# A hybrid block on one Trainium2 core: rows turned through memory instead of through TensorE in the scan stage

## The chip, the core and the metric

The kernel runs on one core of a Trainium2 chip. The core has five engines with instruction streams of their own: PE (TensorE: matrix products into the PSUM memory), DVE (VectorE), ACT (ScalarE), POOL (GpSimd) and SP (SyncE, which here only issues DMAs). Each engine takes its instructions in the order in which the compiled program holds them; they meet through semaphores. SP and POOL issue the DMAs, each on a queue of its own, and 16 DMA engines carry both.

The metric is the device time of one execution in microseconds (us). Ten runs of the kernel before took 1613.59 to 1618.41 us, with a median of 1616.53 us.

## What is computed

Eight sequences of 512 tokens of width 256 pass four sublayers, each added to its input after a layer norm: a linear scan, a mixture of experts, a causal attention with 16 heads, and the same mixture again.

```python
x = x + scan(layernorm(x), Win, bin_, Bp, Cp, Dp, Wout, bout)
x = x + mixture(layernorm(x), router_w, bias, gate_w, up_w, down_w, sh_gate_w, sh_up_w, sh_down_w)
x = x + attention(layernorm(x), Wqkv, Wout)
x = x + mixture(layernorm(x), ...)
# scan:    xi = silu(x @ Win + bin_);  h = 0.9 * h + xi * Bp;  y = sum(h * Cp) + Dp * xi;  y @ Wout + bout
# mixture: scores = sigmoid(x @ router_w.T); the best 2 of 4 groups, of them the best 4 of 16 experts;
#          sum over those experts of weight * (silu(x @ gate) * (x @ up)) @ down, plus two experts that all tokens use
```

## The kernel before

**Stages.** The kernel runs four stages one behind the other: `stretch(Scan())`, `routed(0, ...)`, `stretch(Attention())` and `routed(1, ...)`. A stretch computes a sequence layer for all eight sequences, routes its result to the experts and computes the shared experts beside it; `routed` then runs the routed experts in blocks of 128 rows. The change touches the first stretch.

**Steps of the scan stretch.** A loop over `b` handles one sequence per step. Step `b` interleaves, on the engines, work on four different sequences:

- `layer.main(b, ...)`: the scan of sequence `b`. Eight pairs of products give `pz` (L563) from the turned rows `xT`, ACT and DVE make the states and `y` from it, and `add_projection` (L510, L519) multiplies by the output matrix and adds to the tile `x`.
- For the next sequence, `nxt = b + 1`: its load, its layer norm (`norm(nxt)`, DVE writes `xn`, L493), and `turn(nxt)`, which puts the normalised rows into the turned layout `xT` that the next step's `main` starts from.
- For the sequence before, `b - 1`: `start_route` stores `x` to memory (L1444), `r.norm()` writes its normalised rows into a tile of sorted rows (`sorted_m`, L493), `r.scores()` turns them, makes the router logits (`pl`, L669) and the scores, and `r.rest` goes on: five picks up to the choice `sel` (L739), the prefix product over tokens `pr` (L747, L748), the places and the weights of each choice, and 16 indirect DMAs by POOL (L798) that send rows to their experts' regions. `r.rest` runs on into the next step: its prefix product and the two pieces behind it stand at 0.10, 0.14 and 0.18 of step `b + 1`, the sends after them.
- For the sequences further back: a share of the two shared experts (`experts(layer.quota[...])`, L1146, L1174); 10 of 12 pieces of a sequence per step.

**Order.** `beside(...)` merges these pieces: every piece yields how much of its columns it has used, and the piece that is furthest behind goes next. `timed(steps, *places)` lets the steps of a piece start at given shares of the step (0 to 1). So a place is a share of the PE columns of the step, and sets the order of the text. The framework's compile-time planner then makes each engine's order from the text, with its own expectation of when each operand is there; on the chip that order is fixed, and an engine whose next instruction lacks an operand stands still. `tc.issue_after(...)` adds an order on one engine.

**Two ways of turning rows.** `turned` (L418 to L433) uses PE: for each half of the width four products with the identity matrix (128x128, L430) into one PSUM bank, and a copy of the bank to a tile, which the scan gives to ACT (L432). `by_shares` (L435 to L456) goes by way of memory: SP writes the rows (512 KB) to a DRAM tile `through` (L440), waits for that to land, reads them back in four DMAs of 128 KB (L443), arranged such that the blocks of 32x32 stand where a transposition of blocks alone makes the whole transposition, and DVE turns them in two instructions (L452). If `into_rows` is true the read comes into the tile that was written from; else into another tile of the pool `kb4`, of which there are nine. Before the change only the attention stretch uses `by_shares`, through these two lines, one in `turn` and one in the loop:

```python
if i == 1 and b >= layer.ahead:
    return by_shares(lambda: xn.pop(b), f"l{i}_{b}", lambda xnT: xT.update({b: xnT}), True)
...
timed(r.scores(i == 1), *scores[:2], *spread(*scores[2:], NT)),
```

**SP's queue in a step.** Besides the store of `x`, SP issues the load of a sequence that is needed later (`load_x`, L149), which takes the buffer of sequence `b - 1` (the pool has three) as soon as DVE has read that for `sorted_m`; behind it, by `issue_after`, in steps 2 to 5 six loads of expert weights of 256 KB each (L235 to L237) and one of zeros; and the sum of the shared experts of a sequence (L1184).

**The last step and the tail.** In step 7 the route of sequence 6 has tighter places (`last_rows`, `last_scores`), its picks stand at 0.57 to 0.76, and its prefix product and the two pieces behind it at 0.79, 0.81 and 0.83. After the loop the tail routes sequence 7: 20 pieces of the shared experts, the last four sends of sequence 5, the sends of sequence 6 from 0.16 on, the norm, scores and choice of sequence 7; then the rest of the shared experts beside the last sends and the table of expert blocks (`blocks`).

Of the kernel before, what the change touches and what calls it, by code (L numbers as in the profile page):

```python
# [19 lines left out]
NT = T // P  # L20
# [11 lines left out]
EG, TKG, TK = 4, 2, 4  # L32
# [50 lines left out]
def tile_hybrid_block(  # L83
# [276 lines left out]
    def behind(*pieces):  # L360
        def steps():
            for piece in pieces:
                yield from piece.steps

        return Piece(sum(piece.columns for piece in pieces), steps())
# [17 lines left out]
    def timed(steps, *places):  # L383


        def scaled():
            now = 0
            for place in places:
                yield place - now
                now = place  # L390
                next(steps)
            for _ in steps:
                pass

        return Piece(1, scaled())

    def spread(first: float, last: float, many: int):
        return [first + (last - first) * k / many for k in range(many)]

    def some(steps, many: int):  # L400

        for _ in range(many):
            yield next(steps)

    def issue(piece):
        for _ in piece.steps:
            pass
# [51 lines left out]
    by_scalar = (nc.scalar.copy, nc.scalar.copy)  # L459
# [60 lines left out]


    class Scan:
        mixture, ahead, copies, turns = 0, 1, by_scalar, (0.75, 0.79)
        quota = (10, 10, 20)
        over, sent, begun_last = 4, 0, 4
        early = 0


        norms, scores, choose = (0.08, 0.2, 0.32, 0.4), (0.53, 0.57, 0.65, 0.69), (0.71, 0.97)
        last_rows, last_scores = (0.26, 0.33), (0.43, 0.46)  # L530

        def load(self, b: int):
# [667 lines left out]
    class Attention:  # L1200
        mixture, ahead, copies, turns = 1, 2, by_both, (0.65, 0.85)
        quota = (10, 8, 20)
        over, sent, begun_last = 0, 4, 8
        early = 2
        norms, scores, choose = (0.0, 0.12, 0.2, 0.28), (0.29, 0.45, 0.55, 0.6), (0.66, 0.95)
        last_rows, last_scores = (0.2, 0.28), (0.35, 0.38)
# [214 lines left out]
    def stretch(layer):  # L1421


        i = layer.mixture
        xT, xn, made, routes, sends = {}, {}, {}, {}, []
# [6 lines left out]
            return normed(b, f"l{i}_{b}", place, False, first)  # L1432

        def turn(b: int, copies=layer.copies):
            if i == 1 and b >= layer.ahead:
                return by_shares(lambda: xn.pop(b), f"l{i}_{b}", lambda xnT: xT.update({b: xnT}), True)
            return turned(lambda: xn.pop(b), f"l{i}_{b}", lambda xnT: xT.update({b: xnT}), copies)

        def project(b: int):
            made[b], piece = layer.project(b, xT.pop(b))  # L1440
            return piece
# [12 lines left out]
        def experts(many: int):  # L1454
            return Piece(many * each, some(whole, many))
# [39 lines left out]
        def start_route(b: int):  # L1495
            routes[b] = Route(i, b, layer.copies)
            store(b)
            return routes[b]
# [4 lines left out]
        for b in range(1 if begun else 0, B):  # L1503
            pieces = [begun or layer.main(b, made.pop(b))]
            begun = None
            nxt, last = b + layer.ahead, b == B - 1
            scores, choose, turns = layer.scores, layer.choose, layer.turns
            if i == 0 and b == 1:

                scores, choose, turns = (0.95, 0.955, 0.97, 0.975), (0.98, 0.99), (0.96, 0.965)  # L1510
            fill = []
            if layer.ahead > 1 and not last:
                fill.append(project(b + 1))
            if b > 1:
                shared_sum = experts(layer.quota[last])
                fill.append(shared_sum)
                if len(sends) > 1:
                    pieces.append(timed(sends.pop(0), *spread(0.0, 0.16, layer.over)))
                wait = 0.16 if i == 0 and b == 2 else 0.0
                first = [wait + place for place in (0.1, 0.14, 0.18)]  # L1520
                if layer.over:
                    pieces.append(timed(some(sends[0], 3 + NT * TK - layer.over), *first, *spread(0.22 + wait, 0.97, NT * TK - layer.over)))
                else:
                    pieces.append(timed(sends.pop(), *first, *spread(0.22, 0.66 if last else 0.86, NT * TK)))
            if fill:
                pieces.append(behind(*fill))
            if b > 0:
                r = start_route(b - 1)
                if last:
                    pieces.append(timed(r.norm(), *spread(0.0, 0.12, NT), *spread(*layer.last_rows, NT)))  # L1530
                else:
                    first, then, rows, full = layer.norms
                    pieces.append(timed(r.norm(), *spread(first, then, NT), *spread(rows, full, NT)))
                sends.append(r.rest)
                if last:
                    pieces += [
                        timed(r.scores(), *layer.last_scores, *spread(0.5, 0.56, NT)),
                        timed(some(r.rest, PICKS), *spread(0.57, 0.67, PICKS - 1), 0.76),
                        timed(some(r.rest, 3 + layer.sent), 0.79, 0.81, 0.83, *spread(0.85, 1.0, layer.sent)),
                    ]  # L1540
                else:
                    pieces += [
                        timed(r.scores(i == 1), *scores[:2], *spread(*scores[2:], NT)),
                        timed(some(r.rest, PICKS), *spread(*choose, PICKS)),
                    ]
            if nxt < B:
                added = layer.load(nxt)
                if added is not None:
                    pieces.append(timed(added, 0.31, 0.34))
                stats = 0.36 if added is not None else 0.32  # L1550
                pieces += [
                    timed(norm(nxt), *spread(stats, 0.44, NT), *spread(0.56, 0.64, NT)),
                    timed(turn(nxt), *turns),
                ]
            issue(beside(*pieces))
            if layer.ahead == 1 and nxt < B:
                issue(project(nxt))
            if i == 0 and b == 2:
                for make in pending:
                    make()  # L1560
# [4 lines left out]
        r = start_route(B - 1)  # L1565
        chain = 3 + PICKS
        many = layer.begun_last
        left = [timed(sends.pop(0), *spread(0.0, 0.14, layer.over))] if layer.over else []
        within = (0.16, 0.8) if layer.over else (0.0, 0.5)
        issue(  # L1570
            beside(
                experts(layer.quota[2]),
                timed(r.norm(by_vector=True), *spread(0.0, 0.05, 2 * NT)),
                *left,
                timed(sends.pop(), *spread(*within, NT * TK - layer.sent)),
                timed(r.scores(), 0.2, 0.22, *spread(0.28, 0.33, NT)),
                timed(some(r.rest, chain + many), *spread(0.36, 0.68, chain), *spread(0.84 if layer.over else 0.7, 1.0, many)),
            )
# [11 lines left out]
    with banks_of(one=8):  # L1590
        table = stretch(Scan())
        wqkv_sb, wo_sb = load_attention_weights()
# [95 lines left out]
```

## Time and profile before

| | us |
|---|---|
| median of 10 runs | 1616.53 |
| the profiled execution: its time | 1616.26 |
| its span, from the first to the last instruction | 1614.5 |
| scan stretch: PE's last shared-expert product ends at | 333.3 |
| first product of the routed experts starts at | 334.5 |
| PE busy in the span | 1570.2 |
| DVE busy in the span | 1002.3 |
| ACT, POOL busy in the span | 780.2, 773.6 |

The profile gives, for one execution, the busy time of each engine, what ended each idle time, and the instructions in order of time. PE's matrix products are pipelined: the distance between the starts of two groups of products tells more of the cost of a group than the mean duration of one product. Where a line names a releaser, this is the event that came last by the record. The granted clock of TensorE was 0.989 of full speed over the span, and 1.00 in steps 3 to 7 of the scan.

The starts of the steps can be read from the stores of `x` on SP's queue (L1444): 52.57 us for step 2, then 88.98, 122.73, 158.13, 190.99 and 226.33 us for steps 3 to 7, and 261.06 us for the tail.

### The profile page before, as it was taken

The page shows a single profiled execution, that of the slowest core. Times are in us where ns is not written, and L with a number is a line of the kernel's source. Part 1 is how long each engine was busy: PE and PEld are TensorE (multiplying, and loading weights), DVE is VectorE, ACT ScalarE, POOL GpSimd, SP SyncE. Part 2 cuts the span into 40 slices and gives each one's busy share as a digit, 9 for nine tenths or more (in the row PEclk, how much of TensorE's full clock was granted, in tenths as well). Part 3 has the DMA queues.
Part 4 walks back from the last instruction along what each step waited for, and adds up shares of the span by engine and source line. Part 5 has one row for each costly group of instructions (what it writes and reads, how often), then busy time and mean ns, then how long its engine had stood idle before and what let it go on. Part 6 is the DMA issues. An engine that isn't in the chain of part 4 may idle for free. (4 is left out here: it accounts for less than half of the span.)

```text
span 1614.5 us, 34092 instructions
## 1 busy us (share of the span) xinstructions
PE 1570.2 (97%) x10030; PEld 1159.3 (72%) x10030; DVE 1002.3 (62%) x3264; ACT 780.2 (48%) x1622; POOL 773.6 (48%) x639
## 2 busy tenths in 40 slices
PE   9999999999999999999899999999999999999996
PEld 6566666689999999983444454544558999999995
DVE  6887765344467444437888988878744444544453
ACT  3343443245555555546544554454124555555553
POOL 4376655635556555550014432433533555555554
PEclk9999999999999999999999999999999999999998
DMA  5354424557777776641223434343745767787776
GB/s 172 131 200 153 147 99 141 178 97 104 123 125 107 101 100 96 92 67 49 77 84 101 141 97 117 100 123 101 274 149 92 106 114 130 119 136 132 138 135 133
DMA packets 282765, 196.88 MB, mean 122 GB/s; under 512 B 168688, under 2 KB 262672, under 8 KB 282576
## 3 DMA queue, kind: packets, MB, share of 16 engines
q1 hardware_dynamic: 230016, 121.50, 29.7%
q0 software_dynamic: 51984, 72.09, 25.2%
q8 instruction: 85, 1.39, 0.4%
q10 hardware_dynamic: 576, 1.05, 0.2%
q14 instruction: 104, 0.85, 0.2%
HBM read 91.29 MB, written 103.23 MB: 120 GB/s over the span
## 5 line engine op out<-in xcount | busy, mean ns | idle before, releaser
L1073 POOL DMA_INDIRECT part<-rows x272 | 426.7, 1569 | 341.2 <-ACT rows L1072 245.8
L798 POOL DMA_INDIRECT xg<-sorted_m,slots_m x256 | 269.7, 1053 | 244.1 <-ACT slots_m L795 119.0
L1033 PEld LDWEIGHTS ph<-rows,gate 128*128 128x128 f32 x2160 | 277.6, 191 | 32.7 <-ACT rows L1016 22.6
L1033 PE MATMUL ph<-rows,gate 128*128 128x128 f32 x2160 | 291.7, 278 | 0.5 <-ACT rows L1016 0.5
L1033 PE MATMUL ph<-rows,up 128*128 128x128 f32 x2160 | 285.3, 275 | 0.0
L1063 PE MATMUL pyr<-w_all,rows 128*128 x1088 | 279.5, 380 | 1.4 <-DVE rows L1043 1.4
L1033 PEld LDWEIGHTS ph<-rows,up 128*128 128x128 f32 x2160 | 262.9, 192 | 0.0
L1006 DVE COPY up<-w_all 128x512 f32 x270 | 119.1, 442 | 226.2 <-PE ph L1033 212.7
L1006 ACT COPY gate<-w_all 128x512 f32 x270 | 166.4, 617 | 123.7 <-PE ph L1033 120.0
L1043 DVE TENSOR_TENSOR rows<-ph,rows 128x256 f32<-128x256 f32 x272 | 115.4, 424 | 155.8 <-PE ph L1033 142.6
L1295 ACT ACTIVATE w_all<-ps_a 128x1024 f32<-128x1024 f32 x160 | 155.2, 1022 | 105.4 <-PE ps_a L1285 101.3
L1063 PEld LDWEIGHTS pyr<-w_all,rows 128*128 128x128 f32 x1088 | 186.8, 192 | 15.8 <-DVE rows L1043 1.6
L1072 ACT ACTIVATE rows<-pyr,gain 128x256 f32<-128x256 f32 x272 | 128.9, 474 | 78.5 <-PE pyr L1063 61.7
L1041 ACT ACTIVATE rows<-ph 128x256 f32<-128x256 f32 x272 | 104.6, 384 | 117.2 <-PE ph L1033 101.9
L1174 PE MATMUL pd_m<-sd_sb,act_m 128*128 128x256 f32 x512 | 119.8, 383 | 2.2 <-DVE act_m L1165 1.3
L1174 PEld LDWEIGHTS pd_m<-sd_sb,act_m 128*128 128x128 f32 x512 | 96.1, 191 | 26.5 <-issue 8.8
L1285 PE MATMUL ps_a<-w_all 32*128 32x384 f32 (+3 forms) x1024 | 103.4, 467 | 11.2 <-ACT w_all L1295 11.1
L1305 DVE SCALAR_TENSOR_TENSOR w_all<-w_all,causal 128x512 f32<-128x512 f32 (+1 forms) x160 | 91.6, 573 | 26.4 <-ACT w_all L1295 25.4
L1146 PE MATMUL pg_m<-w_all,su_sb 128*128 128x512 f32 x192 | 92.6, 605 | 0.0
L1285 PEld LDWEIGHTS ps_a<-w_all 32*128 32x128 f32 x1024 | 45.1, 186 | 65.8 <-ACT w_all L1295 37.2
L1146 PE MATMUL pg_m<-w_all,sg_sb 128*128 128x512 f32 x192 | 92.3, 602 | 0.0
L1321 PE MATMUL po_a<-w_all,v_a 128*32 128x512 f32 (+3 forms) x1024 | 89.3, 450 | 0.0
(222 smaller groups left out, 1918.8 us busy)
## 6 DMA issues: line engine op xcount, KB each, us to landing
rows<-xg SPq DMA_DIRECT2D x720, 32.0 KB
rows<-xg SPq DMA_DIRECT2D x92, 134.0 KB
part<-x SPq DMA_DIRECT2D x16, 512.0 KB
w_all<-in_L_ffn_gate_w_dram SPq DMA_DIRECT2D x29, 256.0 KB
w_all<-in_L_ffn_up_w_dram SPq DMA_DIRECT2D x29, 256.0 KB
w_all<-in_L_ffn_down_w_dram SPq DMA_DIRECT2D x29, 256.0 KB
part<-ys_m SPq DMA_DIRECT2D x14, 512.0 KB
sum<-part SPq DMA_DIRECT2D x14, 512.0 KB
```

Source lines behind the costliest of these rows:

```text
L798: nc.gpsimd.indirect_dma_start(out=xg[i], out_offset=bass.IndirectOffsetOnAxis(ap=slots[:, at : at + 1], axis=0), in_=rows[:, t, :], in_of ...
L1006: copy(here, w_all[:, bass.ds(held[n][0] + half * KD * F, KD * F)])
L1033: nc.tensor.matmul(ph[s][:, f * P : (f + 1) * P], lhsT=both[s][:, k * F + f * P : k * F + (f + 1) * P], rhs=rows[:, ROW + k * P : ROW + (k ...
L1041: nc.scalar.activation(act, ph[0], AF.Silu)
L1043: made = nc.vector.tensor_mul(act, ph[1], act)
L1063: nc.tensor.matmul(py, lhsT=act[:, f * P : (f + 1) * P], rhs=w_all[:, bass.ds(w + 2 * KD * F + f * D, D)], start=(f == 0), stop=(f == KF - 1),
L1072: nc.scalar.mul(y, py, gain[:, TK : TK + 1])
L1073: acc = nc.gpsimd.indirect_dma_start(out=parts[i][n % 2], out_offset=bass.IndirectOffsetOnAxis(ap=rows[:, D + 2 * TK : D + 2 * TK + 1].bit ...
L1146: made = nc.tensor.matmul(dst, lhsT=w[:, k, f * P : (f + 1) * P], rhs=xnT[:, k, :], start=(k == 0), stop=(k == KD - 1),)
L1174: nc.tensor.matmul(py[:, j, :], lhsT=acts[n][:, f, t * P : (t + 1) * P], rhs=shared[n][3][:, f, :], start=(n == 0 and f == 0), stop=(n == ...
L1285: nc.tensor.matmul(ps[j // 2][:, j % 2, col : col + n], lhsT=k_sb[w][r, o, c * P : (c + 1) * P], rhs=q_sb[r, o, c * P : T], start=True, st ...
L1295: nc.scalar.activation(es[two], ps[two], AF.Exp, scale=ATT_SCALE)
```

## The change

Five edits, all of which act on the scan stretch alone:

- `turn(b)` uses `by_shares` from `b = layer.through` on: 3 in the scan (so sequences 3 to 7), 2 in the attention, which is what it was there.
- `r.scores(...)` in steps 2 to 6 (routes 1 to 5) uses `by_shares`; the route of sequence 6 in step 7, of sequence 7 in the tail and of sequence 0 in step 1 stay with `turned`.
- The scan's places: `turns` from (0.75, 0.79), which were the two halves on PE, to (0.66, 0.92), which are the DMAs and DVE's two instructions; `scores` from (0.53, 0.57, 0.65, 0.69) to (0.42, 0.64, 0.69, 0.73): the DMAs, DVE's instructions, and the logits; `choose` from (0.71, 0.97) to (0.75, 0.98).
- In step 7 the prefix product of sequence 6 and the two pieces behind it are taken out (a layer with `sent = 0` has no such piece), and
- they stand in the tail, at 0.06, 0.08 and 0.10, ahead of the sends of sequence 6.

```diff
     class Scan:
-        mixture, ahead, copies, turns = 0, 1, by_scalar, (0.75, 0.79)
+        mixture, ahead, copies, turns = 0, 1, by_scalar, (0.66, 0.92)
...
+        through = 3
         early = 0
-        norms, scores, choose = (0.08, 0.2, 0.32, 0.4), (0.53, 0.57, 0.65, 0.69), (0.71, 0.97)
+        norms, scores, choose = (0.08, 0.2, 0.32, 0.4), (0.42, 0.64, 0.69, 0.73), (0.75, 0.98)
...
         def turn(b: int, copies=layer.copies):
-            if i == 1 and b >= layer.ahead:
+            if b >= layer.through:
                 return by_shares(lambda: xn.pop(b), f"l{i}_{b}", lambda xnT: xT.update({b: xnT}), True)
...
                         timed(some(r.rest, PICKS), *spread(0.57, 0.67, PICKS - 1), 0.76),
-                        timed(some(r.rest, 3 + layer.sent), 0.79, 0.81, 0.83, *spread(0.85, 1.0, layer.sent)),
                     ]
+                    if layer.sent:
+                        pieces.append(timed(some(r.rest, 3 + layer.sent), 0.79, 0.81, 0.83, *spread(0.85, 1.0, layer.sent)))
                 else:
                     pieces += [
-                        timed(r.scores(i == 1), *scores[:2], *spread(*scores[2:], NT)),
+                        timed(r.scores(i == 1 or b > 1), *scores[:2], *spread(*scores[2:], NT)),
...
+        early = () if layer.sent else (0.06, 0.08, 0.1)
...
-                timed(sends.pop(), *spread(*within, NT * TK - layer.sent)),
+                timed(sends.pop(), *early, *spread(*within, NT * TK - layer.sent)),
```

More of the change, by code (lines that the diff above doesn't have):

```diff
@@ L1203, in tile_hybrid_block @@
         over, sent, begun_last = 0, 4, 8
+        through = 2
         early = 2
```

## The prediction

> **What bounds the kernel now.** First the page's slices: which engine is full in the scan stretch (0 to 333 us, the first eight of 40 slices).
>
> ```profile
> PE   9999999999999999999899999999999999999996
> DVE  6887765344467444437888988878744444544453
> DMA  5354424557777776641223434343745767787776
> ```
>
> PE is full throughout; DVE comes next in the scan with 6 to 8 tenths. Then the busy time by step, cut at the stores of x; steps 4 and 5 (columns: length, then busy PE, weight loads, DVE, ACT, POOL; granted clock; DMA share; GB/s):
>
> ```profile
> 122.70:158.10 35.40, 35.40 (x144) 22.98 (x143) 25.69 (x87) 14.57 (x36) 22.70 (x23) 1.00 0.45 154
> 158.10:191.00 32.90, 32.90 (x139) 21.83 (x137) 25.15 (x87) 14.65 (x36) 23.39 (x23) 1.00 0.51 171
> ```
>
> PE has no idle time, so what leaves PE shortens the step, if nothing new makes PE wait. A step is about 34 us (122.73 to 190.99, the stores of steps 4 and 6, halved). Third, step 4 in order of time (start, duration, engine, line):
>
> ```profile
> 136.55 0.74 DVE L578 SCALAR_TENSOR_TENSOR y_s<-state_s,bc_sb,xi_s 128x512 f32<-128x512 f32 x1
> 137.22 0.73 DVE L493 TENSOR_SCALAR sorted_m<-x,mv_m,rstd_m 128x256 f32<-128x256 f32 x2
> 137.97 0.38 SPq L149 DMA_DIRECT2D x<-in_L_attn_a_x_dram  x1
> ...
> 140.89 1.10 PE L430 MATMUL pt_m<-ident,sorted_m 128*128 128x128 f32 x8
> ...
> 141.83 1.89 PE L510 MATMUL py_s<-w_scan,y_s 128*128 128x256 f32 x8
> 141.88 0.51 SPq L351 DMA_DIRECT2D part<-zeros  x1
> ...
> 145.37 0.65 PE L669 MATMUL pl_m<-w_all,rw_sb 128*32 128x128 f32 x16
> ...
> 149.49 1.12 PE L430 MATMUL pt_l<-ident,xn 128*128 128x128 f32 x8
> ...
> 150.45 1.89 PE L510 MATMUL py_s<-w_scan,y_s 128*128 128x256 f32 x8
> ```
>
> Three things are to be seen. One turning costs PE 141.83 - 140.89 = 0.94 us (150.45 - 149.49 = 0.96 for the other): 0.95 us. The logits start 145.37 - 137.95 = 7.4 us after the sorted rows are done; steps 3 and 5 give the same (103.85 to 111.28, 171.86 to 179.47). And the load of x starts in the very moment the sorted rows are done, with seven more DMAs behind it until 142.39. Fourth, what the other way of turning takes in the attention stretch, in the route of sequence 6, with no load ahead of the write:
>
> ```profile
> 1053.09 0.40 DVE L493 TENSOR_SCALAR sorted_m<-x,mv_m,rstd_m 128x256 f32<-128x256 f32 x1
> 1053.52 0.36 SPq L440 DMA_DIRECT2D through_m<-sorted_m  x1
> 1056.44 1.91 SPq L443 DMA_DIRECT2D share_m<-through_m  x4
> ...
> 1064.00 1.31 DVE L452 STREAM_TRANSPOSE w_all<-share_m 128x512 f32<-128x512 f32 x2
> ```
>
> Write to read is 2.9 us. Where one load of 512 KB was issued just ahead of the write, it is longer, 997.86 to 1003.44 or 5.6 us, and 780.23 to 787.53 or 7.3 us the first time; there DVE stood idle until the rows had come, 792.48, so first read to rows is 4.95 us. Last, how busy the DMA engines are behind the load of step 4:
>
> ```profile
> 140.00:142.00 2.00, 2.00 (x12) 1.49 (x11) 1.45 (x3) 1.52 (x5) 1.51 (x2) 1.00 1.03 326
> 148.00:150.00 2.00, 2.00 (x9) 1.08 (x8) 2.00 (x5) 0.00 (x0) 1.97 (x4) 1.00 0.99 364
> 150.00:152.00 2.00, 2.00 (x14) 1.82 (x13) 2.00 (x10) 1.26 (x4) 1.57 (x2) 1.00 0.02 4
> ```
>
> They are full from 140 to 150 us. This is the stretch of time in which the new transfers would have to run.
>
> **Part 1, PE.** Ten turnings go (sequences 3 to 7, routes 1 to 5): 10 x 0.95 = 9.5 us less. Waits just ahead of turnings go too: 2.0 us before the one of route 1 (74.98 us). The attainable gain is thus 9.5 to 11.5 us.
>
> [...] The rows above say 0.95 in fp32 and in a stream, and the sum goes by them.
>
> **Part 2, ACT and DVE.** ACT loses 20 copies of 0.59 us (L432), which is free relief. DVE gains 20 instructions of 0.67 to 0.70 us (L452 in the attention): 2.8 us in a step, 13.8 in all. DVE has 35.4 - 25.7 = 9.7 and 32.9 - 25.2 = 7.7 us idle in the steps shown, 5.0 in step 2 (36.4 less 31.4), so I cost this at nothing; if that cover is not where it is needed, the bound is the whole 13.8.
>
> **Part 3, SP and DMA.** Each turning adds a write (0.4 to 0.5 us of SP) and four reads (1.9 us): 50 DMAs, 24 us of SP, 10 MB. SP's time is hidden, it mostly waits. But a read stands on SP until its write has landed, and behind it stand the stores, loads and the other turning's write: the two turnings of a step run one behind the other.
>
> **Part 4, the router's way.** Without other traffic the rows are ready 0.4 + 2.9 + 4.95 + 1.4 (two DVE instructions) = 9.7 us after the sorted rows, against 7.4 for the logits now; the later place of the logits (0.69 for 0.65) gives 0.04 x 34 = 1.4 us back. So they are late by about 1 us. With the burst of steps 2 to 5: the load of x and the write wait for the same instruction, and the loads stand first in the text, as the attention's load does before its write in each step. The write is issued 4.4 us after the sorted rows, the engines are free after 150.1 - 138.0 = 12.1, then 0.5 MB at about 370 GB/s (1.4) and a landing (0.5 to 1.5), then 4.95 and 1.4: about 20.5 us. The other way to it: 2.1 MB is four times the load that made 2.9 into 5.6, so 4 x 2.7 = 10.8 more than 9.7. Both say 20.5, and 8.7 (7.4 + 1.4) is what the place allows: the logits are 1 us late without and 12 us late with the burst.
>
> What of this PE feels depends on how far the planner's order already lets other products go ahead. In the attention DVE's instructions stand 11.5 us after the sorted rows (997.43 to 1008.95; likewise in four steps), so the plan counts on some 13 us up to the logits. That leaves 7.5 us in which PE stands still before the logits of a burst step; none if it expects the burst, 12 if it goes by the place. I take 5.4, less than the plan's distance gives, because part of the loads may slip behind the write. What is late next is the choice: logits to choice takes 11.3 us (146.1 to 157.4), the prefix product stands 5 us behind it in the next step (162.49), so that cushion is gone as well; PE is then ahead of DVE by nothing.
>
> [...]
>
> **Part 5, the scan's own turning.** xn is ready 143.1, the next step's first product needs it at 157.3: 14 us for 9.7. In a burst step the write waits behind the reads of the router's rows and comes some 5 us late, but that lies beside the 5.4 of part 4; I count 0, bounds 0 and 5 per step.
>
> **Part 6, the prefix product moved.** PE waits 0.9 us for the choice of sequence 6 (254.38); that goes. In the tail the three pieces stand some 8 us later; their weights are then ready about when the sorted rows of sequence 7 come now (271.6), which wait 4.0 us for the last scatters of sequence 5. I count -0.9, with 0 to +4 as the other bound.
>
> **Sum.** Steps 2 to 5: 4 x (5.4 - 1.9) = +14. Step 6, where only two expert loads stand ahead: -1.9 + 2 = 0. Step 7: -0.9. Rounded for some overlap, +12 on the profiled 1616.26 us, 0.3 below the median: **1628.5 us**. With the bounds 0 and 8.9 for the stall (12 less the cushion in PE's order) this case alone gives 1619 to 1641.
>
> **The rivals.** *A: the transfers are early enough (faster).* SP's order has the write ahead of the expert loads, or the planner counts them in and fills the time with other products; then PE has 9.5 + 0.9 less and five times some 1 us more: -6 to -9, **1609.5 us**. For it: DVE found its rows landed in eleven of twelve turnings of the attention, and PE there did not wait. Against it: the burst and the equal releaser. It decides where the write stands within two loads of the sorted rows.
>
> *B: DVE becomes the bound (slower).* 28.5 of 32 us leaves little, and `act_m` and `y_s`, for which PE waits, queue behind transpositions that wait for rows. If lateness passes on one for one: 13.8 - 9.5 = +4.4, **1621 us**. Against it: 8 to 10 us idle per step.
>
> *C: no change.* POOL's last scatter ends at 323.2 and the first routed product starts at 334.5, next to the end of PE's shared experts; if POOL's 36 sends of the tail hold that end, PE's 9.5 us buy nothing: **1616.5 us**. Against it: 272 to 323 holds 33 sends at 1.27 us, 42 of 51 us, so they can follow.
>
> **Chances.** The forecast 0.45, A 0.38, B 0.10, C 0.07. Faster by over 0.2% (3.2 us, about what a measurement tells from no change): 0.38; within: 0.07; slower: 0.55. The range must reach to A: 1607 to 1637 leaves out the top of the forecast's own range and the best of A, some 0.17.
>
> **What would show it.** Right: in steps 2 to 5 SP issues L440 behind L237; read issues come 10 us or more after the write; PE stands still before L669 for DVE's L452, and the steps are 36 to 39 us long. Wrong: the write ahead of the loads or no idle time ahead of L669, and steps of 32 us: then A. If DVE's idle time is gone and PE waits at L1174 or L510, B. If the stores of x come 8 us earlier at the tail but the first routed product doesn't, C.

## The result and the profile after

The changed kernel takes 1690.2 us (median of 8 runs, 1686.8 to 1692.86), the kernel before 1617.06 us in the same comparison: ratio 1.0451, 95% interval 1.044 to 1.0463. That is 73 us slower. The prediction had the sign and the mechanism of the larger part, and a sixth of the size: +12 us, 1628.5 us.

The profiled execution has a span of 1685.3 us, at a mean granted clock of 0.97 (0.989 before). The slices of its page show where the time is:

```profile
PE   8766678999999999999999999999999999999996
DVE  6855556653446654443888888987863445544443
PEclk9978879999999999999999999999999999999998
DMA  5435554364777776664132334333654767777776
```

TensorE (PE) is no longer full in the first seven slices, and its clock is at 0.7 to 0.8 in the third to the sixth. Behind them nothing has changed but the place. By step (steps 3, 4 and 2, cut at the stores of x; columns as in the prediction):

```profile
104.30:155.70 51.40, 35.86 (x120) 20.58 (x119) 29.44 (x111) 14.14 (x34) 23.37 (x23) 0.87 0.47 145
155.70:207.00 51.30, 35.88 (x126) 21.98 (x125) 28.57 (x91) 12.39 (x32) 23.07 (x23) 0.83 0.48 149
54.80:104.30 49.50, 31.78 (x110) 18.23 (x109) 32.18 (x121) 11.98 (x28) 16.57 (x19) 0.83 0.50 155
```

Such a step takes 50 to 51 us where it took 33 to 36; PE is busy for 32 to 36 of them, and VectorE (DVE), with all that it has gained, for 29 to 32: neither is the bound, something is waited for. The waits of PE up to 420 us, costliest first (total, times, longest):

```profile
PE pl_m L670 <- DVE w_all L452: 55.2, 5, 17.4
PE pz_s L564 <- DVE xT_l L452: 13.0, 5, 3.3
PE pt_l L430 <- DVE xn L493: 5.1, 4, 3.5
PE pt_m L430 <- DVE sorted_m L493: 1.8, 2, 1.2
```

(The lines of the changed text lie one or two further on: L670 is the logits, L564 the scan's first products, L452 the transpositions.) Now step 3 in order of time. SP's queue:

```profile
126.67 0.37 SPq L149 DMA_DIRECT2D x<-in_L_attn_a_x_dram  x1
127.10 0.56 SPq L235 DMA_DIRECT2D w_all<-in_L_ffn_gate_w_dram  x1
...
131.13 0.45 SPq L440 DMA_DIRECT2D through_m<-sorted_m  x1
138.87 2.16 SPq L443 DMA_DIRECT2D share_m<-through_m  x4
141.13 0.43 SPq L440 DMA_DIRECT2D through_l<-xn  x1
145.08 2.26 SPq L443 DMA_DIRECT2D xn<-through_l  x4
```

DVE, which waits for the rows before it turns them:

```profile
125.59 1.05 DVE L493 TENSOR_SCALAR sorted_m<-x,mv_m,rstd_m 128x256 f32<-128x256 f32 x3
...
144.08 1.30 DVE L452 STREAM_TRANSPOSE w_all<-share_m 128x512 f32<-128x512 f32 x2 [6.01 <-DMA share_m<-through_m]
```

and PE, with the first products of step 4 at the end:

```profile
129.91 1.88 PE L1147 MATMUL pg_m<-w_all,sg_sb 128*128 128x512 f32 x4
131.63 1.89 PE L510 MATMUL py_s<-w_scan,y_s 128*128 128x256 f32 x8
145.53 1.08 PE L670 MATMUL pl_m<-w_all,rw_sb 128*32 128x128 f32 x16 [12.01 <-DVE w_all L452]
146.54 3.21 PE L1147 MATMUL pg_m<-w_all,su_sb 128*128 128x512 f32 x4
149.58 1.89 PE L510 MATMUL py_s<-w_scan,y_s 128*128 128x256 f32 x8
...
158.79 3.34 PE L564 MATMUL pz_s<-xT_l,w_scan 128*128 128x512 f32 x4 [2.16 <-DVE xT_l L452]
161.92 2.28 PE L1175 MATMUL pd_m<-sd_sb,act_m 128*128 128x256 f32 x8
```

Three readings. The sorted rows are done at 126.6, when the load of x is issued; the write stands behind the load and seven more issues, its landing takes 7.7 us instead of the attention's 2.9, and the logits start at 145.5, 18.9 us after the sorted rows. Between these two PE has products for only 18.9 - 12.0 = 6.9 us. And the group of four products of 128x512 behind each of the two waits takes 3.21 and 3.34 us in place of 1.88.

The same for the other steps (rows sorted to logits; PE idle; products in between): step 2 18.7, 17.4, 1.3; step 4 20.6, 13.3, 7.3; step 5 19.6, 11.2, 8.5. Step 6, with no load ahead: 12.5, 1.4, 11.1 us.

**The balance.** The first routed product starts at 405.6 us, 334.5 before: 71.1 us later, nearly the whole loss. The waits of PE that the list names sum to 79.0 us up to there, 11.9 before: +67.1. The products behind the four long waits for logits and the five for the scan's rows take 8.2 and 8.5 us longer than elsewhere (a group of four of 128x512 otherwise takes 1.88 us, of eight of 128x256 1.89, the logits 0.64): +16.7. The ten turnings: -9.5. Sum +74.3, some 3 us more than the shift; the kernel before has slow products of this kind too (see the last section), and they are not taken off here.

### The profile page after: what moved, and what is told of

It is laid out like the page before. It is cut to its first block, busy times and chain, and to the rows that moved or that the text cites. A ratio compares the mean times of both kernels' runs of the same rounds, so it can differ in the third digit from the quotient of the medians.

```text
span 1685.3 us, 34015 instructions
## 1 busy us (share of the span) xinstructions
PE 1574.9 (93%) x9950; PEld 1154.7 (69%) x9950; DVE 1017.3 (60%) x3284; ACT 768.9 (46%) x1602; POOL 769.9 (46%) x639
## 5 line engine op out<-in xcount | busy, mean ns | idle before, releaser
L1034 PEld LDWEIGHTS ph<-rows,gate 128*128 128x128 f32 x2160 | 277.5, 191 | 33.0 <-ACT rows L1017 22.5
L1073 ACT ACTIVATE rows<-pyr,gain 128x256 f32<-128x256 f32 x272 | 128.7, 473 | 78.4 <-PE pyr L1064 61.7
L1147 PE MATMUL pg_m<-w_all,su_sb 128*128 128x512 f32 x192 | 97.7, 633 | 0.0
```

Of the source, the lines that this page charges most:

```text
L1034: nc.tensor.matmul(ph[s][:, f * P : (f + 1) * P], lhsT=both[s][:, k * F + f * P : k * F + (f + 1) * P], rhs=rows[:, ROW + k * P : ROW + (k ...
L1073: nc.scalar.mul(y, py, gain[:, TK : TK + 1])
L1147: made = nc.tensor.matmul(dst, lhsT=w[:, k, f * P : (f + 1) * P], rhs=xnT[:, k, :], start=(k == 0), stop=(k == KD - 1),)
```

## The experiments

Each time stands beside the kernel before, run with it; ratios with 95% intervals. Beside e13 to e16 the kernel before itself took 1636 us, on another chip than the others; there only the ratios are compared. "The trip" is the way through memory: write, read and DVE's transpositions.

**What each part does alone.** First (e2) the router's turning alone; the scan's own is by PE as before, and the prefix product is not moved:

```diff
-        mixture, ahead, copies, turns = 0, 1, by_scalar, (0.66, 0.92)
+        mixture, ahead, copies, turns = 0, 1, by_scalar, (0.75, 0.79)
...
-        through = 3
+        through = B
```

> Only the routes 1 to 5 are turned through memory; sequences 3 to 7 are turned by PE at their old places, and the prefix product stands where it stood. Theory: the router's rows carry the loss: PE stands still 50 to 60 us before the logits and works some 8 to 10 us longer at half clock, less 5 us of products: 1665 to 1682 us. Rival (the loss comes from two ways through memory one behind the other on SP): below 1645 us.

Measured: 1668.89 us, ratio 1.0326 [1.031, 1.0342], +52 us, as the theory had it. PE waits 53.1 us for the logits' rows, and not once for the scan's. Then (e3) the scan's own turning alone; the router's rows are turned by PE, at the old places:

```diff
-                        timed(r.scores(i == 1 or b > 1), *scores[:2], *spread(*scores[2:], NT)),
+                        timed(r.scores(i == 1), *scores[:2], *spread(*scores[2:], NT)),
```

> Only the sequences 3 to 7 are turned through memory, the routes by PE at their old places, the prefix product where it stood. Theory: 14 us from xn to its first use cover the way through memory even behind the loads but for 0 to 3 us a step, and 5 us of products are gone: 1610 to 1622 us. Rival (the loads delay this turning as much as the other): 5 us or more per step with the half clock behind it, 1635 us or more.

Measured: 1642.62 us, ratio 1.0159 [1.0139, 1.0178], +26 us; PE waits 18.9 us for the scan's rows, behind the step without a load of `x` too (2.2 us there). The theory (1610 to 1622 us) missed; the time is in the rival's range, with waits of 2.2 to 6.5 us. And (e4) the prefix product alone, moved in the kernel before:

```diff
-                        timed(some(r.rest, 3 + layer.sent), 0.79, 0.81, 0.83, *spread(0.85, 1.0, layer.sent)),
...
+        early = () if layer.sent else (0.06, 0.08, 0.1)
...
-                timed(sends.pop(), *spread(*within, NT * TK - layer.sent)),
+                timed(sends.pop(), *early, *spread(*within, NT * TK - layer.sent)),
```

> The kernel before with the prefix product of sequence 6 moved to the tail. Theory: 0.9 us of waiting goes and nothing else moves: 1614 to 1618 us. Rival (the sends of sequence 6 and the rows of sequence 7 come later and hold the end of the stretch): 1619 to 1624 us.

Measured: 1615.84 us, ratio 0.9995 [0.9984, 1.0006]: no change. The two turnings make the loss, 52 + 26 us alone and 73 together.

**The burst.** The expert loads and the zeros of steps 2 to 5 (those of step 1 too) go behind the store of x instead of behind the load of x, so that only that load stands ahead of the write; once in the changed kernel (e1), once in the kernel before as a control (e5):

```diff
+                if b > 1:
+                    with tc.issue_after(stored[-1].ins):
+                        for load in later[b - 1 :: shares]:
+                            load()
+                    load_x(b + 1)
+                    return
                 with tc.issue_after(load_x(b + 1).ins):
```

> The changed kernel, but in steps 2 to 5 the expert weights and zeros are issued right behind the store of x at the start of the step; only the load of x stays ahead of the write of the router's rows. Theory (the loads ahead of the write on SP's queue): the rows come some 12 to 13 us after the sorted rows instead of 18.5, PE's idle time before the logits falls from 11 to 17 us to 4 to 8 us per step, the time to 1655 to 1670 us. Rival (the compiled order puts the logits 4 us behind the sorted rows, and the way through memory alone is the cost): idle time stays at 9 us or more per step, 1675 to 1690 us. Rival (the loads are all of it): within 5 us of the kernel before.

> The kernel before with the expert loads of steps 2 to 5 issued behind the store of x. Theory (there the loads are in nobody's way): 1614 to 1620 us, within 0.2% of the kernel before. Rival (the place of the loads costs or gains by itself): outside of it, and the runs with early loads must be read against this one.

Measured: 1662.06 us, ratio 1.0287 [1.0262, 1.0311]; the control 1615.52 us, ratio 0.9992 [0.9983, 1.0001]; both times as the theories had them (of the waits for logits one, 12.3 us, is above the theory's 4 to 8). So 28 of the 73 us come from the loads ahead of the write, and 46 do not. The waits, and SP in step 3, of the changed kernel with the loads moved:

```profile
PE pl_m L678 <- DVE w_all L452: 29.7, 5, 12.3
PE pz_s L572 <- DVE xT_l L452: 12.9, 5, 3.3
```

```profile
120.82 0.38 SPq L149 DMA_DIRECT2D x<-in_L_attn_a_x_dram  x1
121.24 0.57 SPq L440 DMA_DIRECT2D through_m<-sorted_m  x1
126.64 2.15 SPq L443 DMA_DIRECT2D share_m<-through_m  x4
```

From write to read is 5.4 us now, as with one load ahead in the attention (5.6). Together with the changed kernel's own rows it grows with what was issued ahead of the write: 3.3 us with nothing ahead (step 6, 276.66 to 279.98), 5.4 behind 0.5 MB, 7.7 to 8.6 behind 2 MB (steps 2 to 5). No run shows whether the write waits for the loads or merely shares the DMA engines with them. The logits still wait 29.7 us, since PE's order has too few products between; the waits for the scan's rows have not moved at all.

**The half clock.** Idle products, whose result nobody reads, ahead of the logits of routes 1 to 4 in the changed kernel, to keep PE busy during the wait: first 90 (e6), which the profile shows as 180 of 0.11 us, 20.3 us; later 45 (e12), 10.2 us.

```diff
+                if self.i == 0 and self.b < 5:
+                    keep_busy(90, f"wait_{self.b}")
                 yield from logits(self.i, self.b, self.tag, self.held)
```

> The changed kernel with 90 products of ones by ones (128 columns, some 0.11 us each, 10 us) on PE ahead of the logits of routes 1 to 4; they fill the idle time and their result is not used. Theory (after an idle time of some us TensorE's clock is granted at half for a while, 1.7 us lost behind each wait): granted clock 1.00 behind the logits, 7 us less: 1680 to 1686 us. Rival (the slow products behind a wait come from something else, as the full DMA engines): no gain, 1690 us or more, since fillers can only delay.

> The changed kernel with 45 idle products (some 10 us by the run with 90) ahead of the logits of routes 1 to 4. Theory (the products behind a wait run at half clock because TensorE stood idle): the wait ahead of the logits falls from 55 us to some 15, the four logits' share of the half-clock loss, 4 to 8 us, goes, and the time is 1680 to 1687 us at a clock of 0.98 or more. Rival (the half clock there comes from the full DMA engines): the filled time runs at half clock too, and the time is 1690 us or more.

Measured: 1712.71 us, ratio 1.0598 [1.0578, 1.0618], and 1697.03 us, ratio 1.0496 [1.0481, 1.0511]. Both theories missed, and the times lie in the rivals' ranges: four times 20.3 us are more than the waits they could fill, and 45 left waits of 4.7 to 7.5 us, with slow groups behind them. The first answers the question all the same. A window of step 2 that the filler takes (last columns: granted clock, DMA share, GB/s), and PE behind it:

```profile
77.00:97.00 20.00, 18.64 (x160) 18.08 (x158) 1.32 (x3) 0.00 (x0) 7.46 (x9) 1.00 0.81 257
```

```profile
97.73 0.64 PE L672 MATMUL pl_m<-w_all,rw_sb 128*32 128x128 f32 x16 [2.08 <-DVE w_all L452]
98.30 1.98 PE L1149 MATMUL pg_m<-w_all,su_sb 128*128 128x512 f32 x4
100.12 1.89 PE L510 MATMUL py_s<-w_scan,y_s 128*128 128x256 f32 x8
```

The DMA engines are as full as in the changed kernel's step 2 (0.87 from 81 to 93 us, at clock 0.50), yet the clock is 1.00 and the group behind takes 1.98 us, not 3.44. The filler of e12 tells the same (72 to 84 us: clock 1.00, DMA engines 0.80 full), and so does the changed kernel without any filler: behind the wait at 108.5 us the products run at a clock of 0.53 while the DMA engines stand idle (108.6 to 111.7 us, share 0.00). So in these stretches the low clock went with PE's idle time, not with the traffic. The times add up: 81 us of filler less 51.8 us of waits (55.2 to 3.4) would be +29; it is +22.5 against the changed kernel, although the waits for the scan's rows grew from 13.0 to 16.6 us. So 7 us or more of slow products went; 8.2 were counted above.

**Why the scan's rows are late.** First (e7) only the second place of the scan's turning, in the changed kernel:

```diff
-        mixture, ahead, copies, turns = 0, 1, by_scalar, (0.66, 0.92)
+        mixture, ahead, copies, turns = 0, 1, by_scalar, (0.66, 0.8)
```

> The changed kernel with DVE's part of the scan's own turning at 0.80 of the step instead of 0.92. Theory (its rows had been there for 8 us; DVE had the instructions behind the next step's first work, so PE's 13 us before the first products of a step and the 7 us at half clock behind them come from the place): 1668 to 1678 us. Rival (that wait is for the transfer): DVE then stands still for the rows, 1688 us or more.

Measured: 1684.83 us, ratio 1.0426 [1.0406, 1.0446]; the waits fell from 13.0 to 11.9 us; neither the theory (1668 to 1678 us) nor the rival. Next (e9) the scan's turning alone with everything out of its way: place 0.82, expert loads behind the store, the load of x behind the four reads.

```diff
+                        with tc.issue_after(reads[-1].ins):
+                            load_x(b + 1)
```

> Only the scan's own turnings through memory, with nothing ahead of the write: the expert loads behind the store of x, the load of x behind the reads, DVE's part at 0.82. Theory (PE's work less 5 x 0.95 us and no wait in its place): 1610 to 1614 us. Rival (DVE, or the later load of x, makes PE wait all the same): 1617 to 1630 us.

Measured: 1632.23 us, ratio 1.0099 [1.0083, 1.0115], and PE still waits 14.1 us. The rival was right in kind, 2 us above its range; DVE in step 3 shows what it is (the reads were issued from 118.11 on; with the attention's 4.95 us the rows were there at about 123, an estimate):

```profile
126.05 0.58 DVE L758 TENSOR_REDUCE sel_m<-pick_m 128x64 f32<-128x256 f32 x1
126.55 0.68 DVE L522 TENSOR_TENSOR x<-py_s,x 128x512 f32<-128x512 f32 x1
127.26 0.75 DVE L471 BATCH_NORM_STATS2 stats_m<-x 128x6 f32<-128x256 f32 x2
...
128.35 0.69 DVE L1184 TENSOR_TENSOR act_m<-pg_m,sig_m 128x512 f32<-128x512 f32 x1
128.96 1.29 DVE L455 STREAM_TRANSPOSE xT_l<-xn 128x512 f32<-128x512 f32 x2
```

No DMA is waited for: DVE takes up the transpositions behind the choice, the addition into x and the next norm's statistics, and PE's last product of the step had ended at 127.8. So the order was changed by hand (e10), the last addition into x of a step behind the transpositions:

```diff
-            nc.vector.tensor_add(rows, py, rows)
+            with tc.issue_after(own.pop().ins) if own and half == 1 and tag[0] == "s" else nullcontext():
+                nc.vector.tensor_add(rows, py, rows)
```

> The scan's own turning alone, as in the run with the loads and the load of x out of its way (1632.2 us, PE waits 14.1 us for the turned rows), with one more order on VectorE: the last addition into x of a step stands behind the two transpositions of the next sequence's rows. Theory (the wait is VectorE's order: the rows have landed some 5 us before it comes to them, behind the addition and the statistics): the waits ahead of the scan's first product fall from 14.1 us to under 2, the 1.7 us that each of the five loses behind it at half clock go too, and with five turnings less on TensorE the time is 1608 to 1614 us. Rival (the rows or the engine are late whatever the order is, and the wait moves to the addition, the store or the logits): 1625 us or more.

Measured: 1622.86 us, ratio 1.0043 [1.0026, 1.006]; the waits for these rows fell to 6.2 us (0.45 to 2.2 us each). Of the 26 us of e3, 11 went with the loads and the place (e9) and 9 with this one line of order; 6 are left, between the theory's 1608 to 1614 us and the rival's 1625. Ahead of its transpositions in step 3 DVE now stands for a product of PE's:

```profile
123.39 0.69 DVE L1188 TENSOR_TENSOR act_m<-pg_m,sig_m 128x512 f32<-128x512 f32 x1 [0.82 <-PE pg_m L1169]
124.00 1.29 DVE L455 STREAM_TRANSPOSE xT_l<-xn 128x512 f32<-128x512 f32 x2
```

With the transpositions ahead of the choice's last instructions too, and their place at 0.72 (e16):

```diff
-        mixture, ahead, copies, turns = 0, 1, by_scalar, (0.66, 0.82)
+        mixture, ahead, copies, turns = 0, 1, by_scalar, (0.66, 0.72)
...
-        nc.vector.tensor_tensor(
+        with tc.issue_after(own[-1].ins) if own and i == 0 else nullcontext():
+          nc.vector.tensor_tensor(
             pick,
```

> The scan's own turning alone, as in the run with the transpositions ahead of the last addition into x (ratio 1.0043; waits for the turned rows of 0.45 to 2.2 us), and the transpositions ahead of the last instructions of the choice as well, where the rows have landed by that run's trace. Theory (the rest of that run's loss is the place in VectorE's order): the waits ahead of the scan's first product are under 1 us in all, and the time is 2 to 7 us under the kernel before of the same call. Rival (what the transpositions push back in VectorE's order, the choice, the addition into x and the statistics behind it, costs as much as the waits did): 3 us above the kernel before or more, with waits for sorted_m, the choice or the states in place of those for the turned rows.

and with the whole trip early in the step, from step 2 on (e14, against e10 like e16):

```diff
-                    timed(norm(nxt), *spread(stats, 0.44, NT), *spread(0.56, 0.64, NT)),
-                    timed(turn(nxt), *turns),
+                    timed(norm(nxt), *(spread(stats, 0.44, NT) + spread(0.56, 0.64, NT) if i or b < 2 else spread(0.0, 0.06, NT) + spread(0.07, 0.14, NT))),
+                    timed(turn(nxt), *(turns if i or b < 2 else (0.16, 0.5))),
```

> The scan's own turning alone, a step ahead: the norm of the next sequence at 0.0 to 0.14 of the step, its trip at 0.16, its transpositions right behind the logits on VectorE, far ahead of the first product that needs them; loads as in the run with the transpositions first (1622.9 us, waits of 0.45 to 2.2 us for these rows). Theory (the wait is order alone): no wait for the turned rows from sequence 4 on, TensorE's 4.75 us for five turnings are saved, and the time is 1608 to 1614 us. Rival (VectorE, with 2.8 us more in each step, makes other products wait, as those for the sorted rows, y or the choice): 1617 us or more.

Measured: ratio 1.006 [1.0043, 1.0077] and 1.011 [1.0093, 1.0126]. Both theories missed, and what the rivals foretold came. In e14 the list of PE's waits names no rows turned by DVE; it has 10.8 us for `sorted_m`, 7.5 for the choice and 7.1 for `act_m` (4.3, 0.9 and 1.3 in the profile of before, though on another chip). In e16 it has 4.6 us for the scan's rows, 7.1, 5.5 and 3.3 for these three: what is put early on DVE makes others late.

**The whole change in a better order.** In e11 (this diff is against the changed kernel) the same loads as in e9; the norm of the next sequence at 0.02 to 0.26 and its trip at 0.28 (from step 3 on), the addition pinned as above, the logits at 0.84, the choice at 0.88, the prefix product at 0.22 of the next step:

```diff
-        norms, scores, choose = (0.08, 0.2, 0.32, 0.4), (0.42, 0.64, 0.69, 0.73), (0.75, 0.98)
+        norms, scores, choose = (0.08, 0.2, 0.32, 0.4), (0.42, 0.76, 0.84, 0.87), (0.88, 1.0)
-                first = [wait + place for place in (0.1, 0.14, 0.18)]
+                first = [wait + place for place in ((0.22, 0.25, 0.28) if i == 0 else (0.1, 0.14, 0.18))]
```

> The whole change (scan's and router's rows turned through memory, the prefix product in the tail) with its places and loads set anew: expert loads behind the store of x, the load of x behind the reads, the norm of the next sequence at 0.02 to 0.26 of the step and its trip at 0.28, its transpositions ahead of the last addition into x; the logits at 0.84 (about seven groups of products behind the sorted rows instead of two to four), the choice at 0.88 to 1.0, the prefix product at 0.22 of the next step. Theory (the 68 us of waits and the half clock behind them come from an order that leaves TensorE nothing to do during the trip of some 10 us, not from the trip itself): TensorE's waits up to 420 us are under 10 us, and the time is 1606 to 1618 us. Rival (the ring from logits to choice, prefix product, weights, sorted rows, trip and logits again is longer than the 34 us of a step, whatever the places): TensorE waits 3 to 6 us per step, ahead of the prefix product or the logits, and the time is 1630 to 1660 us.

Measured: 1636.01 us, ratio 1.0125 [1.0111, 1.014]: 19 us of loss instead of 73, with the ten turnings still on DVE, the trip still through memory and the waits for logits down from 55.2 to 9.6 us:

```profile
PE pl_m L692 <- DVE w_all L455: 9.6, 4, 3.4
PE pz_s L586 <- DVE xT_l L455: 7.7, 1, 7.7
PE pt_m L432 <- DVE sorted_m L499: 5.8, 3, 3.9
PE py_s L516 <- DVE y_s L601: 2.7, 3, 1.4
```

So some 54 us of the loss were order and placing, that of the loads included. The time is in the rival's range, though its waits of 3 to 6 us in every step aren't there (four waits for logits, 2.0 to 3.4 us). In e13, against e11, both pairs of transpositions stand ahead of the addition, the logits at 0.88, the norm and trip as in e14, and the last route later:

```diff
-        norms, scores, choose = (0.08, 0.2, 0.32, 0.4), (0.42, 0.76, 0.84, 0.87), (0.88, 1.0)
-        last_rows, last_scores = (0.26, 0.33), (0.43, 0.46)
+        norms, scores, choose = (0.08, 0.2, 0.32, 0.4), (0.42, 0.76, 0.88, 0.9), (0.91, 1.0)
+        last_rows, last_scores = (0.36, 0.43), (0.53, 0.56)
```

> The whole change with a still earlier order. Against the run with all places anew (1636.0 us; TensorE waits some 2 us per step for the router's turned rows, whose transpositions stand behind the second addition into x, 7.7 us for the scan's rows in step 2, 3.9 us in step 7, with slow groups behind each): both transpositions stand ahead of the second addition, the logits one group of products later (0.88), the norm of the next sequence at 0.0 to 0.14 and its trip at 0.16 from step 2 on, the last route's rows and logits at 0.36 to 0.56. Theory (all that the change lost is order: the trip itself fits into a step): the waits ahead of the logits and of the scan's products fall under 4 us together up to 420 us, the first routed product starts at 322 to 334 us, and the time is 1605 to 1616 us, with 1616.5 for the kernel before. Rival (the routing's ring of logits, choice, prefix product, weights, sorted rows and trip fills the whole step, so that a wait taken away here comes back ahead of another product): TensorE still waits 10 us or more in the scan, and the time is 1622 us or more.

Measured: ratio 1.0147 [1.013, 1.0164], no better, and the rival's case: some 40 us of waits. The list names no rows turned by DVE any more, and others head it:

```profile
PE pd_m L1200 <- DVE act_m L1191: 13.5, 4, 5.6
PE py_s L515 <- DVE y_s L604: 12.0, 5, 4.5
PE pt_l L432 <- DVE xn L498: 4.3, 4, 2.5
```

**What DVE's added work costs by itself.** In e15 the kernel before, with 20 transpositions of 128x512 more on DVE (sequences 3 to 7, four each, into a tile that is no longer needed), and no trip:

```diff
             copies[k](dst[:, k, :], flat)
+            if k == KD - 1 and tag in twice:
+                for half in (0, 1, 0, 1):
+                    nc.vector.transpose(
+                        rows.rearrange("p t d -> p (t d)")[:, half * T : (half + 1) * T], dst[:, half, :]
+                    )
```

> The kernel before with work for VectorE that nobody waits for: behind the turning of sequences 3 to 7 by TensorE, four transpositions 128x512 of the turned rows into the tile of the normalised rows, which is no longer needed (20 of 0.67 to 0.70 us, 13.8 us in all, as many as the change adds). Theory (VectorE's idle time of 5 to 10 us per step covers them, as the prediction had it): no change, within 3 us of the kernel before in the same call. Rival (VectorE's order is a ring through choice, weights and sorted rows, and what is put in comes out at its end): 5 to 14 us more, with waits of TensorE for sorted_m, act_m or y_s.

Measured: ratio 1.002 [1.0007, 1.0033], or 3.3 us (1.1 to 5.4) for 13.8 us of work. Nearly covered, not quite: at the edge of the theory's 3 us, below the rival's 5.

No version was found that beats the kernel before.

## Why the prediction was off

**Right.** PE was the bound, and each turning was worth 0.95 us to it. SP's order was as foretold: load of x, weights, zeros, and the write behind them. The rows were turned and the logits came 18.7 to 20.6 us after the sorted rows in the four burst steps; 20.5 was predicted, though with reads 10 us or more after the write, and they came 7.7 to 8.6 us after it. The landing of 0.5 to 1.5 us in that sum is an estimate: in the attention of before the DMA share falls from 0.91 (1055.5 to 1056.0 us) to 0.02 (1056.0 to 1056.5) and the read is issued at 1056.44, and 2.9 us less 1.4 of transfer leave 1.5. That the write moves only when the engines are free of the loads was an assumption; no run shows it. Step 6, for which 2 us were counted, waits 1.4 us; its write went ahead of the two expert loads, not behind them. The prefix product was counted at -0.9 us and does nothing that can be measured (-2.6 to +1.0 us). DVE is not the bound (29 of 51 us busy), and its 13.8 us, counted at nothing, cost 3.3 us by themselves.

**The step that failed: part 4, what PE feels of the lateness.** The prediction had the logits 12 us late by their place, and named 12 as the bound "if it goes by the place". It then took 5.4 us, since in the attention DVE's transpositions stand 11.5 us behind the sorted rows, "so the plan counts on some 13 us"; that left 7.5, and 5.4 was taken because loads might slip behind the write, which none did in these four steps. In the scan it doesn't: PE's order holds 1.3 to 8.5 us of products between sorted rows and logits, about the 8.7 of the place or less. The four stalls were 17.4, 12.0, 13.3 and 11.2 us, 13.5 on average. This term was 4 x 5.4 = 21.6 us and should have been 53.8: 32 us. Its largest value, 12, would have given 1655.8 us; nor do the 1619 to 1641 us of the prediction follow from its bounds of 0 and 8.9, with which the sum gives 1607.8 and 1643.4. The view that would have told was at hand: step 4's order of PE, shown in the prediction, with two groups between turning and logits. The distance was borrowed from another stage, whose steps and order are others.

**Part 5, the scan's own turning, counted 0 (bounds 0 to 5 a step).** It waits 13.0 us in five steps, 2.6 each: inside the bounds, but not in the sum. The time for the transfer was thought of, 14 us for 9.7; the place of the transpositions in DVE's order wasn't. The wait stays when the rows come early (e9, 14.1 us), and more than half of it goes with the order (e10, 6.2 us).

**Not in the prediction at all: the clock.** Each of the nine waits of over 2 us for turned rows is followed by products at a low clock (0.50 to 0.56 granted over the first 3 us, 0.71 behind one of them), some 1.8 us of loss each: 16.7 us.

These three are 32 + 13 + 17 = 62 us; from 1628.5 to 1690.2 are 61.7. That they meet so closely is in part luck: the +12 was rounded from 13, and the balance itself is open by 3 us.

**Rivals.** A, transfers early enough, fell with the order on SP; and e1 shows that without the burst the change would still have cost 46 us. B, DVE as the bound, was wrong as a share of time; but its picture of `act_m` and `y_s`, for which PE waits behind the transpositions, is what e13 shows. C, no change, fell: the first routed product moved with the scan. Whether POOL's sends would have held back a gain is not shown, since there was none.

**What stays open.** Why the whole change stays 1.2 to 1.5% above the kernel before in the new orders (e11, e13), and the scan's turning alone 0.4 to 1.1% (e9, e10, e14, e16). DVE's added work is part of it (3.3 us for all 20 transpositions; the scan's alone are 10), and in e13, e14 and e16 so are waits that move to DVE's other products; a ring of routing (logits, choice, prefix product, weights, sorted rows, logits again), which before takes one step of 34 us, might explain it, but no run measured it by itself. Three of these runs (e13, e14, e16) were made on the chip where the kernel before was slower too.

## What to carry to other kernels

Before work is taken off the busiest engine and sent by a longer way, count in its own order, in the stage itself, how much work stands between the last instruction that makes the operand and the first that needs it; a trip longer than that is idle time (18.9 us against 6.9 of work in step 3 here, 12.0 us idle), whatever the other engines have to spare, and the clock behind such a gap can be low as well (1.5 to 2.7 us for each of the nine here). Look up in the same way what stands ahead of the receiving instruction on the engine that finishes the trip: a transfer that is early gains nothing if the engine comes to it late (14.1 us of waits in e9, 6.2 in e10 with another order). And a small urgent transfer issued by the same instruction as a burst of loads, but behind it, pays for the burst: 28 us here, which one moved wait gave back at no cost to the kernel before.

## What the runs showed of the hardware

In the changed kernel each of the nine waits of PE of 2.16 us or more for turned rows was followed by slow products (the granted clock over the first 3 us is 0.50 behind the four for logits, 0.53 to 0.56 behind four of those for the scan's rows, 0.71 behind the fifth, at 260.3 us); behind the one of 1.36 us they were not slow (1.00 from 289.1 to 292.1 us). From the timeline of PE, the logits of step 6, and the scan's rows at 210 us against them:

```profile
289.10 0.64 PE L670 MATMUL pl_m<-w_all,rw_sb 128*32 128x128 f32 x16 [1.36 <-DVE w_all L452]
289.68 1.99 PE L510 MATMUL py_s<-w_scan,y_s 128*128 128x256 f32 x8
...
210.14 3.43 PE L564 MATMUL pz_s<-xT_l,w_scan 128*128 128x512 f32 x4 [2.25 <-DVE xT_l L452]
213.36 2.15 PE L1147 MATMUL pg_m<-w_all,sg_sb 128*128 128x512 f32 x4
```

The lengths do not divide so in other runs. In the kernel before, a wait of 1.54 us was followed by slow products (granted clock 0.64 from 272.2 to 277.0 us; the eight of a turning otherwise take 1.10 us, the group of four 1.88), and in e6 one of 3.16 us was not, nor one of 3.15:

```profile
272.12 2.39 PE L430 MATMUL pt_m<-ident,sorted_m 128*128 128x128 f32 x8 [1.54 <-DVE sorted_m L493]
274.31 2.88 PE L1146 MATMUL pg_m<-w_all,su_sb 128*128 128x512 f32 x4
```

```profile
283.01 1.95 PE L564 MATMUL pz_s<-xT_l,w_scan 128*128 128x512 f32 x4 [3.16 <-DVE xT_l L452]
284.80 1.88 PE L1149 MATMUL pg_m<-w_all,sg_sb 128*128 128x512 f32 x4
```

So the length of a wait alone doesn't tell whether the clock falls; what else decides is not shown. Where it fell, a wait of 17.4 us cost 2.0 us behind it, one of 2.25 us 1.8 us: between these two the price hardly depends on the length. The nine waits of the changed kernel cost 16.7 us in this way.
